# A four-layer graph network on one core: leaky slope, row sums, squares, degrees and scaling moved between VectorE, ScalarE and GpSimd, with new settings for the planner

## The chip, the cores and the metric

The kernel runs on one core of a Trainium2 chip. The metric is the device time of one execution in microseconds (us), the median of three runs. The core's engines work side by side, each through its own queue in order: TensorE (PE in the profile) multiplies matrices, VectorE (DVE) does elementwise work and reductions, ScalarE (ACT) evaluates functions with a scale and a bias per partition, GpSimd (POOL) does elementwise work on small or unhurried tiles, and SyncE (SP) issues the transfers (DMA).

## The reference: what is computed

Sixty-four graphs, each with 256 nodes of 512 features (`x`) and a weighted 256x256 adjacency matrix (`adj`), all in float32, pass through four layers. Every layer normalises, rectifies, calls a graph operator and adds the result to x:

```
h = maximum(layernorm(x), 0);  x = x + attention(h, adj, W, a)
h = maximum(layernorm(x), 0);  x = x + gcn(h, adj, kernel, bias)
h = maximum(layernorm(x), 0);  x = x + masked(h, adj, kernel)
h = maximum(layernorm(x), 0);  x = x + sage(h, adj, W)

attention: Wh = h W;  e = leaky_relu(Wh a1 + (Wh a2)^T, 0.2)
           e = where(adj > 0.5, e, -9e15);  softmax;  elu(e Wh)
gcn:       dh = rsqrt(rowsum(adj + I));  relu(dh (adj+I) dh h kernel + bias)
masked:    relu(adj h kernel) * (any nonzero in the row of h's input)
sage:      relu([h, (adj h) / max(rowsum(adj), 1e-6)] W^T)
```

## The kernel before, in words

A graph fills two chunks of 128 partitions: `xs` holds x (128 x 2 x 512), `aT` the transposed adjacency matrix, `a_nat` the matrix as it lies in memory, from which the degrees are summed. The 64 graphs are independent, and several are under way at once.

**The planner.** The kernel isn't written in the order in which it runs. `graph(b)` records every instruction of a graph with `op(engine, us, function, reads, writes)`, where `us` is the author's duration for it. `Plan.add` multiplies this by the factor of its engine in `STRETCH` (L25). `Plan.place` (L69) then lays all recorded instructions out on a model of the engines and of the buffers: each has a due time, counted back from the due time of its graph (`APART` = 12 for each graph, L23 and L343) along what depends on it; an engine takes, of the instructions that can start soonest, an urgent one first and then the one that is due first. For PE, an instruction counts as ready only `SPARE` = 0.8 us after its inputs (L26, L110). `emit` writes the queues in the order of the starts in that layout. On the chip the queues run in this fixed order with the true durations; an instruction whose inputs are late holds up all that is behind it on its engine. SP's queue, with the transfers in it, is ordered in the same way.

**The stages of a graph.** `norm(l)` (L372) opens each layer: two `bn_stats` and `bn_aggr` on DVE (L381, L383), `rstd` by an addition and a power on POOL (L385, L387), in layer 1 a product with `dh` on DVE (L390), `nb` = -mean times rstd on DVE (L392), and two Relu on ACT that write `h` (L396). `aggregate` (L424) multiplies h with the adjacency matrix or the attention into PSUM (`pt`). `left_sums` and `more_sums` build seven operands `xw` from it, and `project` (L485) multiplies them with seven prepared weights `wb` in a seven-product scheme with three PSUM banks (`pz`, `py`, `pv`; all at L503). Between products ACT copies bank z out (`snap`, L542) and DVE adds the others (L544). `pieces` lists the three parts in which the result comes, and `elu0`, `relu_add` and `masked` add them to `xs` on DVE.

Layer 0 has a stage of its own ahead of `aggregate`: four products with row sums on DVE (L590) give the logits `lg`, `along` brings one of them to all partitions through memory (`pl`, two dependent transfers), ACT adds the other (`e`, L596), and then come the leaky slope (L603), the mask as a product (L605) and as an addition of `off` (L607), the maximum (L610), the exponential with its sum (L614), the reciprocal (L617) and the scaling by it (L620). Degrees are summed on DVE (L576).

Layer 3 transposes h by 32x32 blocks on DVE (`hb`, L722) and brings the blocks into place by 16 transfers on SP (`hw`, L727) before it multiplies.

The order of emission starts with the weights; the last one (`last_weight`, L306) is transposed on PE (L325), copied out of PSUM by ACT (L332), and its sums are made on POOL (L289).

Of the kernel before, what the change touches and what calls it, by code (L numbers as in the profile page):

```python
# [11 lines left out]
ALU = mybir.AluOpType  # L12
AX = mybir.AxisListType

P = 128
# [6 lines left out]
HOP = 0.25  # L22
APART = 12.0  # L23

STRETCH = {"DVE": 1.06, "ACT": 1.1, "POOL": 1.1, "PE": 1.0, "DMA": 1.0}  # L25
SPARE = 0.8  # L26

# [121 lines left out]
def kernel(  # L149
# [39 lines left out]
    class Tiles:  # L189
# [148 lines left out]
    def quarter(t, i, j):  # L338
        return t[:, i, j * OH : (j + 1) * OH]

    def graph(b):

        me = Tiles(str(b), APART * b)  # L343
        op, declare, together = me.op, me.declare, me.together

        def along(name, column, keys):
# [22 lines left out]
        op("DMA", 256, lambda g: nc.sync.dma_start(  # L369
            g["a_nat"], adj[b].rearrange("(c p) m -> p c m", p=P)), (), ["a_nat"])  # L370

        def norm(l, scale=None):  # L372

            st, mv, rs, nb, h = (f"{n}{l}" for n in ("stats", "mv", "rstd", "nb", "h"))
            declare(st, [P, NC, 6], tag="stats")
            declare(mv, [P, NC, 2], tag="mv")
            declare(rs, [P, NC], tag="rstd")
            declare(nb, [P, NC], tag="nb")
            declare(h, [P, NC, F], tag="h")
            for c in range(NC):  # L380
                op("DVE", 0.69, lambda g, c=c: nc.vector.bn_stats(g[st][:, c, :], g["xs"][:, c, :]),  # L381
                   XS[2 * c : 2 * c + 2], [f"{st}.{c}"])
                op("DVE", 0.18, lambda g, c=c: nc.vector.bn_aggr(g[mv][:, c, :], g[st][:, c, :]),  # L383
                   [f"{st}.{c}"], [f"{mv}.{c}"])
            op("POOL", 0.31, lambda g: nc.gpsimd.tensor_scalar_add(g[rs], g[mv][:, :, 1], EPS_LN),  # L385
               [f"{mv}.0", f"{mv}.1"], [rs])
            op("POOL", 0.72, lambda g: nc.gpsimd.tensor_tensor(g[rs], g[rs], minus_half, ALU.pow),  # L387
               [rs, "=half"], [rs])
            if scale is not None:
                op("DVE", 0.2, lambda g: nc.vector.tensor_tensor(g[rs], g[rs], g[scale], ALU.mult),  # L390
                   [rs, scale], [rs])
            op("DVE", 0.3, lambda g: nc.vector.scalar_tensor_tensor(  # L392
                g[nb], g[mv][:, :, 0], -1.0, g[rs], ALU.mult, ALU.mult),
               [f"{mv}.0", f"{mv}.1", rs], [nb])
            for c in range(NC):
                op("ACT", 0.81, lambda g, c=c: nc.scalar.activation(  # L396
                    g[h][:, c, :], g["xs"][:, c, :], AF.Relu, bias=g[nb][:, c : c + 1],
                    scale=g[rs][:, c : c + 1]), XS[2 * c : 2 * c + 2] + [nb, rs], [f"{h}.{c}"])
# [153 lines left out]
        def pieces(l):  # L552
            kept = f"c{l}"
            return (
                (1, "xs.10", lambda g: g[f"pz{l}"], [f"pz{l}"], lambda g: quarter(g["xs"], 1, 0), ["xs.10"], 256),
                (1, "xs.11", lambda g: g[kept][:, 2], [f"{kept}.11"], lambda g: quarter(g["xs"], 1, 1), ["xs.11"], 256),
                (0, "xs.0", lambda g: both(g[kept]), [f"{kept}.00", f"{kept}.01"], lambda g: g["xs"][:, 0, :], ["xs.00", "xs.01"], 512),
            )


# [3 lines left out]
        for q in range(P // Q):  # L564
# [10 lines left out]
        norm(0)  # L575
        op("DVE", 0.67, lambda g: nc.vector.tensor_reduce(g["deg"], g["a_nat"], AX.X, ALU.add),  # L576
           ["a_nat"], ["deg"])
        op("POOL", 0.36, lambda g: nc.gpsimd.tensor_scalar_add(g["dh"], g["deg"], 1.0), ["deg"], ["dh"])
        op("POOL", 0.72, lambda g: nc.gpsimd.tensor_tensor(g["dh"], g["dh"], minus_half, ALU.pow),
           ["dh", "=half"], ["dh"])  # L580
        op("DVE", 0.18, lambda g: nc.vector.tensor_scalar_max(g["rdeg"], g["deg"], EPS_DEG),
           ["deg"], ["rdeg"])
        op("DVE", 0.18, lambda g: nc.vector.reciprocal(g["rdeg"], g["rdeg"]), ["rdeg"], ["rdeg"])
# [11 lines left out]
        for c in range(NC):  # L595
            op("ACT", 0.47, lambda g, c=c: nc.scalar.activation(  # L596
                g["e"][:, c, :], g["pl"], AF.Identity, bias=g["lg"][:, 1, c : c + 1]),
               ["pl", f"lg.1{c}"], [f"e.{c}"], urgent=True)
        E = ["e.0", "e.1"]
        declare("off", [P, NC, N])  # L600
        op("DVE", 0.48, lambda g: nc.vector.tensor_scalar(
            g["off"], g["aT"], 0.5, NEG_INF, ALU.is_le, ALU.mult), ["aT"], ["off"])
        op("DVE", 0.69, lambda g: nc.vector.scalar_tensor_tensor(  # L603
            g["e"], g["e"], ALPHA, g["e"], ALU.mult, ALU.max), E, E)
        op("DVE", 0.69, lambda g: nc.vector.scalar_tensor_tensor(  # L605
            g["e"], g["aT"], 0.5, g["e"], ALU.is_gt, ALU.mult), E + ["aT"], E)
        op("DVE", 0.69, lambda g: nc.vector.tensor_tensor(g["e"], g["e"], g["off"], ALU.add),  # L607
           E + ["off"], E)
        declare("top", [P, NC])
# [9 lines left out]
        for c in range(NC):  # L619
            op("DVE", 0.37, lambda g, c=c: nc.vector.tensor_scalar_mul(  # L620
                g["e"][:, c, :], g["e"][:, c, :], g["den"][:, c : c + 1]),
               [f"e.{c}", f"den.{c}"], [f"e.{c}", "e"])
        aggregate("h0", "e", 0)


        def elu0(i, key, y, y_keys, to, to_keys, n, tag):
# [10 lines left out]
            op("DVE", us, lambda g: nc.vector.scalar_tensor_tensor(  # L637
                to(g), g[ex], -1.0, to(g), ALU.add, ALU.add), [ex] + to_keys, to_keys)

# [28 lines left out]

        def relu_add(i, key, y, y_keys, to, to_keys, n):
            op("DVE", 0.43 if n == 256 else 0.69, lambda g: nc.vector.scalar_tensor_tensor(  # L670
                to(g), y(g), 0.0, to(g), ALU.max, ALU.add), y_keys + to_keys, to_keys,
               urgent="pz3" in y_keys)

        first, second, third = pieces(1)

        def last1(pz):
            declare("v1", [P, OH], tag="ex256")
            op("DVE", 0.49, lambda g: scaled(g, 1, g["v1"], g[pz], 0), [pz, "dh", "=bias"], ["v1"], urgent=True)
            relu_add(1, "xs.10", lambda g: g["v1"], ["v1"], first[4], first[5], 256)

        project([Weighted("xw1", 1)], 1, scaled_keep, 0.49, scaled_total, last1, ["dh", "=bias"])
        relu_add(*second)
        relu_add(*third)
        norm(2)

# [12 lines left out]

        def masked(i, key, y, y_keys, to, to_keys, n, tag):
# [5 lines left out]
            op("DVE", 0.43 if n == 256 else 0.69, lambda g: nc.vector.tensor_tensor(  # L705
                to(g), g[v], to(g), ALU.add), [v] + to_keys, to_keys)

# [53 lines left out]
        for at, to, i in ((2, S3, 1), (3, S4, 0)):  # L761
# [3 lines left out]
        project([Weighted("hw", 3), Gathered("aT", "aw", "y")], 3, plain_keep, 0.38, plain_total,  # L765
                lambda _: relu_add(*pieces(3)[0]))
        _, second, third = pieces(3)
        relu_add(*second)
        relu_add(*third)
        op("DMA", 512, lambda g: nc.sync.dma_start(  # L770
# [9 lines left out]
    for b in range(B):  # L780
        graph(b)
    buffers = dict(
        xs=7, a_nat=1, ab=1, aT=6, h=3, mva=6, xw=5, c=3, off=1, junk=1, ex256=2, ex512=2,
        wa_col=1, turned=1, row=4, pl=2, pr=1, hb=1, ps=8,
    )
    for tag in ("stats", "mv", "rstd", "nb", "deg", "dh", "rdeg", "lg", "top", "den", "mask"):
        buffers[tag] = 6
# [34 lines left out]
```

## Time and profile before

| | us |
|---|---|
| median of the runs (lowest, highest) | 2857.97 (2857.74, 2859.51) |
| the profiled execution's own time | 2858.11 |
| its span, first to last instruction | 2856.3 |
| PE busy | 2807.5 (98% of the span) |
| DVE busy | 2317.2 (81%) |
| ACT busy | 1326.1 (46%) |
| POOL busy | 1098.4 (38%) |

The busy time of an engine says how much of the span it worked, not who waited for whom. Where one engine is full over a stretch, work of the others in that stretch is hidden behind it as long as it comes in time; where it isn't, the row of what it waited for names the releaser. A matmul of this kernel (128x128 by 128x256, float32) appears as two records.

### The profile page before, as it was taken

What the parts mean: (1) busy time and instruction counts of PE and PEld (TensorE: products, weight loads), DVE (VectorE), ACT (ScalarE), POOL (GpSimd) and SP (SyncE); (2) the same over time, 40 slices, a digit from 0 to 9 for tenths busy, and PEclk for the clock granted to TensorE, in tenths of its full rate; (3) what the DMA queues carried; (4) which work ended last, traced back from release to release, by engine and by line L of the source; (5) the groups of instructions that cost most, each with busy time, mean ns of one, the idle gap of its engine ahead of it and who ended that gap; (6) DMA issues with size and microseconds to landing.
All of it is one profiled execution on the core that took longest, in us unless ns stands there. A gap on an engine that the chain in (4) does not pass through costs nothing.

```text
span 2856.3 us, 41700 instructions
## 1 busy us (share of the span) xinstructions
PE 2807.5 (98%) x12968; PEld 2464.4 (86%) x12968; DVE 2317.2 (81%) x5904; ACT 1326.1 (46%) x2963; POOL 1098.4 (38%) x1691
## 2 busy tenths in 40 slices
PE   4999999999999999999999999999999999999998
PEld 3888888888888888888888888888888888888887
DVE  8888888888888888878888878888888888888764
ACT  4544444444454444444444444444444445444432
POOL 5443343343333433433433334434334344344331
PEclk9999999999999999999999999999999999999999
DMA  6122222222222222222222222222222222222111
GB/s 184 22 48 51 55 59 49 59 65 47 51 60 54 58 59 49 61 49 56 64 49 53 67 44 57 59 50 59 56 50 62 49 54 66 48 53 61 39 37 45
DMA packets 495052, 160.98 MB, mean 56 GB/s; under 512 B 424816, under 2 KB 460656, under 8 KB 494832
## 3 DMA queue, kind: packets, MB, share of 16 engines
q1 hardware_dynamic: 494832, 158.33, 23.5%
q8 instruction: 104, 1.70, 0.3%
q14 instruction: 116, 0.95, 0.1%
HBM read 90.96 MB, written 33.69 MB: 44 GB/s over the span
## 4 chain that ended last, share of the span: by engine, by line
PE 97%; DVE 1%; SPq 1%; DMA 1%; ACT 0%; issue 0%; POOL 0%; DVEq 0%; ACTq 0%; POOLq 0%
PE pz L503 42%; PE pt L434 23%; PE pv L503 21%; PE py L503 11%; SPq L727 0%; DMA xs<-in_x_dram 0%; DMA wb<-in_L_gnn_W_dram 0%; ACT h L396 0%; DVE e L605 0%; DVE e L607 0%; SPq L567 0%; ACT e L614 0%; DVE stats L381 0%; DVE xs L670 0%; DMA hw<-hb 0%
## 5 line engine op out<-in xcount | busy, mean ns | idle before, releaser
L503 PE MATMUL pz<-wb,xw 128*128 128x256 f32 x3072 | 752.5, 379 | 0.9 <-ACT c L542 0.9
L503 PEld LDWEIGHTS pz<-wb,xw 128*128 128x128 f32 x3072 | 583.4, 190 | 80.7 <-ACT c L542 1.3
L503 PE MATMUL pz<-wb,hw 128*128 128x256 f32 x2048 | 524.5, 379 | 5.8 <-DMA hw<-hb 3.5
L406 POOL TENSOR_TENSOR xw<-xw 128x256 f32<-128x256 f32 x384 | 300.7, 803 | 536.1 <-DVE xw L402 443.3
L542 ACT COPY c<-pz 128x256 f32<-128x256 f32 x576 | 212.8, 370 | 591.7 <-PE pz L503 575.0
L503 PEld LDWEIGHTS pz<-wb,hw 128*128 128x128 f32 x2048 | 388.6, 190 | 60.9 <-issue 3.9
L396 ACT ACTIVATE h<-xs,nb,rstd 128x512 f32<-128x512 f32 x512 | 401.3, 811 | 60.0 <-DVE nb L392 59.9
L503 PE MATMUL pv<-wb,xw 128*128 128x256 f32 x1536 | 394.0, 379 | 0.0
L385 POOL TENSOR_SCALAR rstd<-mv 128x2 f32<-128x2 f32 x256 | 98.3, 384 | 698.2 <-DVE mv L383 325.7
L381 DVE BATCH_NORM_STATS2 stats<-xs 128x6 f32<-128x512 f32 x512 | 340.9, 681 | 6.9 <-DMA xs<-in_x_dram 5.2
L503 PEld LDWEIGHTS pv<-wb,xw 128*128 128x128 f32 x1536 | 291.8, 190 | 39.7
L544 DVE TENSOR_TENSOR c<-pv,c 128x256 f32<-128x256 f32 x384 | 161.0, 420 | 151.5 <-PE pv L503 112.8
L503 PE MATMUL pv<-wb,hw 128*128 128x256 f32 x1024 | 263.7, 380 | 0.0
L434 PE MATMUL pt<-e,h 128*128 128x256 f32 x1024 | 243.0, 382 | 20.9 <-ACT e L596 20.9
L434 PE MATMUL pt<-ahT,h 128*128 128x256 f32 x1024 | 237.5, 382 | 2.9 <-ACT b_w L332 2.9
L434 PE MATMUL pt<-aT,h 128*128 128x256 f32 x1024 | 238.5, 379 | 0.0
L434 PEld LDWEIGHTS pt<-e,h 128*128 128x128 f32 x1024 | 195.6, 191 | 48.7 <-ACT e L596 21.1
L434 PEld LDWEIGHTS pt<-ahT,h 128*128 128x128 f32 x1024 | 196.4, 192 | 30.3 <-ACT b_w L332 3.1
L503 PEld LDWEIGHTS pv<-wb,hw 128*128 128x128 f32 x1024 | 195.1, 191 | 26.7
L542 ACT COPY y<-pz 128x256 f32<-128x256 f32 x192 | 71.2, 371 | 316.4 <-PE pz L503 311.5
L434 PEld LDWEIGHTS pt<-aT,h 128*128 128x128 f32 x1024 | 194.6, 190 | 26.4
L387 POOL TENSOR_TENSOR rstd<-rstd,minus_half 128x2 f32<-128x2 f32 x256 | 200.6, 784 | 21.3
(103 smaller groups left out, 4411.0 us busy)
## 6 DMA issues: line engine op xcount, KB each, us to landing
xs<-in_x_dram SPq DMA_DIRECT2D x64, 512.0 KB
hw<-hb SPq DMA_DIRECT2D x1024, 32.0 KB
out_dram<-xs SPq DMA_DIRECT2D x64, 512.0 KB
ab<-in_adj_dram SPq DMA_DIRECT2D x512, 32.0 KB
a_nat<-in_adj_dram SPq DMA_DIRECT2D x64, 256.0 KB
pl<-dpl SPq DMA_DIRECT2D x64, 128.0 KB
pr<-dpr SPq DMA_DIRECT2D x64, 128.0 KB
w3n_w<-in_L_gnn_W_dram SPq DMA_DIRECT2D x4, 512.0 KB
```

Of the source, the lines that this page charges most:

```text
L381: op("DVE", 0.69, lambda g, c=c: nc.vector.bn_stats(g[st][:, c, :], g["xs"][:, c, :]), XS[2 * c : 2 * c + 2], [f"{st}.{c}"])
L385: op("POOL", 0.31, lambda g: nc.gpsimd.tensor_scalar_add(g[rs], g[mv][:, :, 1], EPS_LN), [f"{mv}.0", f"{mv}.1"], [rs])
L387: op("POOL", 0.72, lambda g: nc.gpsimd.tensor_tensor(g[rs], g[rs], minus_half, ALU.pow), [rs, "=half"], [rs])
L396: op("ACT", 0.81, lambda g, c=c: nc.scalar.activation(g[h][:, c, :], g["xs"][:, c, :], AF.Relu, bias=g[nb][:, c : c + 1], scale=g[rs][:, c ...
L406: op("POOL", 0.85, lambda g, i=i, o=o: nc.gpsimd.tensor_tensor(g[xw][:, o], g[xw][:, i], g[xw][:, S2], ALU.subtract), put(i, S2), put(o), ...
L434: nc.tensor.matmul(g[pt][:, kk, :], lhsT=g[h][:, c, k * P : (k + 1) * P], rhs=g[moving][:, c, :], start=(c == 0), stop=(c == NC - 1),)
L503: nc.tensor.matmul(g[t], lhsT=o.left(g, left, k), rhs=o.right(g, right, k), start=start and n == 0, stop=n == len(parts) - 1, skip_group_c ...
L542: return "ACT", lambda g, to, block: nc.scalar.copy(to, block)
L544: plain_total = (0.43, lambda g, i, to, block: nc.vector.tensor_tensor(to, block, to, ALU.add))
```

## The change: what it does

- **Leaky slope and mask.** The ACT instruction that adds the column now applies the parametric relu with slope 0.2 (L596), and the DVE instruction for the slope is gone. `off` becomes +0.5 or -0.5, and one DVE instruction takes the minimum of e and `off` times 1.8e16: three DVE instructions become one.
- **Row sums.** The DVE instructions that add a layer's result to `xs` also give the row sums of the new x (`accum_out` into `total`, a new tile), in layers 0 to 2. So `norm` of layers 1 to 3 has no `bn_stats` and no `bn_aggr`: POOL makes the negative mean from the sums (two instructions), and ACT squares x minus mean with a row sum (two instructions, whose elementwise result goes into `h` as scratch). Layer 0 keeps `bn_stats`.
- **Small products.** `nb` of layers 1 to 3 and the product with `dh` go from DVE to POOL.
- **Degrees and scaling.** The degrees are summed by two ACT copies with a row sum, `a_nat` written over itself; the attention is scaled by ACT.
- **Planner.** `STRETCH` is 1.25 for DVE, 1.15 for ACT and 1.2 for POOL; `SPARE` is 0.15; the due times of the last two graphs lie 0.3 x 12 us behind the one before each instead of 12. Three buffers for `ex256`, one for `pl`, six for `total`.

```diff
-STRETCH = {"DVE": 1.06, "ACT": 1.1, "POOL": 1.1, "PE": 1.0, "DMA": 1.0}
-SPARE = 0.8
+LAST, LATE = 2, 0.3
+STRETCH = {"DVE": 1.25, "ACT": 1.15, "POOL": 1.2, "PE": 1.0, "DMA": 1.0}
+SPARE = 0.15
...
-        me = Tiles(str(b), APART * b)
+        me = Tiles(str(b), APART * (b - (1.0 - LATE) * max(0, b - (B - 1 - LAST))))
...
+                op("POOL", 0.3, lambda g: nc.gpsimd.tensor_scalar(
+                    g[mv][:, 0, 1:2], g[t][:, 1:2], g[t][:, 2:3], -1.0 / F, ALU.add, ALU.mult),
+                   [f"{t}.10", f"{t}.11"], [f"{mv}.m1"])
+                op("POOL", 0.3, lambda g: nc.gpsimd.tensor_scalar(
+                    g[mv][:, 0, 0:1], g[t][:, 0:1], -1.0 / F, None, ALU.mult), [f"{t}.0"], [f"{mv}.m0"])
+                for c in (1, 0):
+                    op("ACT", 1.0, lambda g, c=c: nc.scalar.activation(
+                        g[h][:, c, :], g["xs"][:, c, :], AF.Square, bias=g[mv][:, 0, c : c + 1],
+                        accum_out=g[mv][:, 1, c : c + 1]),
+                       XS[2 * c : 2 * c + 2] + [f"{mv}.m{c}"], [f"{h}.{c}", f"{mv}.v{c}"])
+                op("POOL", 0.31, lambda g: nc.gpsimd.tensor_scalar(
+                    g[rs], g[mv][:, 1], 1.0 / F, EPS_LN, ALU.mult, ALU.add),
+                   [f"{mv}.v0", f"{mv}.v1"], [rs])
...
+        def into_x(l, key, at, us, fn, reads, to_keys, urgent=False):
+            t = f"total{l + 1}"
+            sums = l < 3
+            op("DVE", us + (0.1 if sums else 0.0), lambda g: fn(
+                g, dict(accum_out=g[t][:, at : at + 1]) if sums else {}),
+               reads + to_keys, to_keys + ([f"{t}.{key}"] if sums else []), urgent=urgent)
...
-        op("DVE", 0.67, lambda g: nc.vector.tensor_reduce(g["deg"], g["a_nat"], AX.X, ALU.add),
-           ["a_nat"], ["deg"])
+        for c in range(NC):
+            op("ACT", 0.66, lambda g, c=c: nc.scalar.activation(
+                g["a_nat"][:, c, :], g["a_nat"][:, c, :], AF.Copy, accum_out=g["deg"][:, c : c + 1]),
+               [f"a_nat.{c}"], [f"a_nat.{c}", f"deg.{c}"])
...
-                g["e"][:, c, :], g["pl"], AF.Identity, bias=g["lg"][:, 1, c : c + 1]),
+                g["e"][:, c, :], g["pl"], AF.Prelu, bias=g["lg"][:, 1, c : c + 1], alpha=ALPHA),
...
-            g["off"], g["aT"], 0.5, NEG_INF, ALU.is_le, ALU.mult), ["aT"], ["off"])
+            g["off"], g["aT"], 0.5, 0.5, ALU.is_gt, ALU.subtract), ["aT"], ["off"])
         op("DVE", 0.69, lambda g: nc.vector.scalar_tensor_tensor(
-            g["e"], g["e"], ALPHA, g["e"], ALU.mult, ALU.max), E, E)
-        op("DVE", 0.69, lambda g: nc.vector.scalar_tensor_tensor(
-            g["e"], g["aT"], 0.5, g["e"], ALU.is_gt, ALU.mult), E + ["aT"], E)
-        op("DVE", 0.69, lambda g: nc.vector.tensor_tensor(g["e"], g["e"], g["off"], ALU.add),
-           E + ["off"], E)
+            g["e"], g["off"], -2.0 * NEG_INF, g["e"], ALU.mult, ALU.min), E + ["off"], E)
...
-            op("DVE", 0.37, lambda g, c=c: nc.vector.tensor_scalar_mul(
-                g["e"][:, c, :], g["e"][:, c, :], g["den"][:, c : c + 1]),
+            op("ACT", 0.5, lambda g, c=c: nc.scalar.activation(
+                g["e"][:, c, :], g["e"][:, c, :], AF.Copy, scale=g["den"][:, c : c + 1]),
                [f"e.{c}", f"den.{c}"], [f"e.{c}", "e"])
```

More of the change, by code (lines that the diff above doesn't have):

```diff
@@ L369, in graph @@
         op("DMA", 256, lambda g: nc.sync.dma_start(
-            g["a_nat"], adj[b].rearrange("(c p) m -> p c m", p=P)), (), ["a_nat"])
+            g["a_nat"], adj[b].rearrange("(c p) m -> p c m", p=P)), (), ["a_nat.0", "a_nat.1"])
         def norm(l, scale=None):
-            st, mv, rs, nb, h = (f"{n}{l}" for n in ("stats", "mv", "rstd", "nb", "h"))
-            declare(st, [P, NC, 6], tag="stats")
-            declare(mv, [P, NC, 2], tag="mv")
+            mv, rs, nb, h = (f"{n}{l}" for n in ("mv", "rstd", "nb", "h"))
+            declare(mv, [P, 2, NC], tag="mv")
             declare(rs, [P, NC], tag="rstd")
@@ L379, in norm @@
             declare(h, [P, NC, F], tag="h")
[L380 to L386, printed above, removed]
+            if l == 0:
+                declare("stats", [P, NC, 6])
+                for c in range(NC):
+                    op("DVE", 0.69, lambda g, c=c: nc.vector.bn_stats(
+                        g["stats"][:, c, :], g["xs"][:, c, :]), XS[2 * c : 2 * c + 2], [f"stats.{c}"])
+                    op("DVE", 0.18, lambda g, c=c: nc.vector.bn_aggr(
+                        g[mv].rearrange("p a c -> p c a")[:, c, :], g["stats"][:, c, :]),
+                       [f"stats.{c}"], [f"{mv}.m{c}", f"{mv}.v{c}"])
+                op("POOL", 0.31, lambda g: nc.gpsimd.tensor_scalar(
+                    g[rs], g[mv][:, 1], EPS_LN, None, ALU.add), [f"{mv}.v0", f"{mv}.v1"], [rs])
+                sign = -1.0
+            else:
+                t = f"total{l}"
+                op("POOL", 0.3, lambda g: nc.gpsimd.tensor_scalar(
[8 more added lines that the diff above has]
+                       XS[2 * c : 2 * c + 2] + [f"{mv}.m{c}"], [f"{h}.{c}", f"{mv}.v{c}"])
+                op("POOL", 0.31, lambda g: nc.gpsimd.tensor_scalar(
+                    g[rs], g[mv][:, 1], 1.0 / F, EPS_LN, ALU.mult, ALU.add),
+                   [f"{mv}.v0", f"{mv}.v1"], [rs])
+                sign = 1.0
             op("POOL", 0.72, lambda g: nc.gpsimd.tensor_tensor(g[rs], g[rs], minus_half, ALU.pow),
@@ L389, in norm @@
             if scale is not None:
-                op("DVE", 0.2, lambda g: nc.vector.tensor_tensor(g[rs], g[rs], g[scale], ALU.mult),
+                op("POOL", 0.3, lambda g: nc.gpsimd.tensor_tensor(g[rs], g[rs], g[scale], ALU.mult),
                    [rs, scale], [rs])
[L392 to L395, printed above, removed]
+            if l == 0:
+                op("DVE", 0.22, lambda g: nc.vector.scalar_tensor_tensor(
+                    g[nb], g[mv][:, 0], sign, g[rs], ALU.mult, ALU.mult),
+                   [f"{mv}.m0", f"{mv}.m1", rs], [nb])
+            else:
+                op("POOL", 0.3, lambda g: nc.gpsimd.tensor_tensor(
+                    g[nb], g[mv][:, 0], g[rs], ALU.mult), [f"{mv}.m0", f"{mv}.m1", rs], [nb])
+            for c in (0, 1) if l == 0 else (1, 0):
                 op("ACT", 0.81, lambda g, c=c: nc.scalar.activation(
@@ L553, in pieces @@
             kept = f"c{l}"
+            if l < 3:
+                declare(f"total{l + 1}", [P, 3], tag="total")
             return (
-                (1, "xs.10", lambda g: g[f"pz{l}"], [f"pz{l}"], lambda g: quarter(g["xs"], 1, 0), ["xs.10"], 256),
-                (1, "xs.11", lambda g: g[kept][:, 2], [f"{kept}.11"], lambda g: quarter(g["xs"], 1, 1), ["xs.11"], 256),
-                (0, "xs.0", lambda g: both(g[kept]), [f"{kept}.00", f"{kept}.01"], lambda g: g["xs"][:, 0, :], ["xs.00", "xs.01"], 512),
-            )
+                (1, "10", lambda g: g[f"pz{l}"], [f"pz{l}"], lambda g: quarter(g["xs"], 1, 0), ["xs.10"], 256, 1),
+                (1, "11", lambda g: g[kept][:, 2], [f"{kept}.11"], lambda g: quarter(g["xs"], 1, 1), ["xs.11"], 256, 2),
+                (0, "0", lambda g: both(g[kept]), [f"{kept}.00", f"{kept}.01"], lambda g: g["xs"][:, 0, :], ["xs.00", "xs.01"], 512, 0),
+            )
+        def into_x(l, key, at, us, fn, reads, to_keys, urgent=False):
[4 more added lines that the diff above has]
+               reads + to_keys, to_keys + ([f"{t}.{key}"] if sums else []), urgent=urgent)
         declare("ab", [P, NC, N], tag="ab")
@@ L575, in graph @@
         norm(0)
-        op("DVE", 0.67, lambda g: nc.vector.tensor_reduce(g["deg"], g["a_nat"], AX.X, ALU.add),
-           ["a_nat"], ["deg"])
-        op("POOL", 0.36, lambda g: nc.gpsimd.tensor_scalar_add(g["dh"], g["deg"], 1.0), ["deg"], ["dh"])
+        for c in range(NC):
+            op("ACT", 0.66, lambda g, c=c: nc.scalar.activation(
+                g["a_nat"][:, c, :], g["a_nat"][:, c, :], AF.Copy, accum_out=g["deg"][:, c : c + 1]),
+               [f"a_nat.{c}"], [f"a_nat.{c}", f"deg.{c}"])
+        op("POOL", 0.36, lambda g: nc.gpsimd.tensor_scalar_add(g["dh"], g["deg"], 1.0), ["deg.0", "deg.1"], ["dh"])
         op("POOL", 0.72, lambda g: nc.gpsimd.tensor_tensor(g["dh"], g["dh"], minus_half, ALU.pow),
@@ L581, in graph @@
         op("DVE", 0.18, lambda g: nc.vector.tensor_scalar_max(g["rdeg"], g["deg"], EPS_DEG),
-           ["deg"], ["rdeg"])
+           ["deg.0", "deg.1"], ["rdeg"])
         op("DVE", 0.18, lambda g: nc.vector.reciprocal(g["rdeg"], g["rdeg"]), ["rdeg"], ["rdeg"])
@@ L619, in graph, with elu0 @@
         for c in range(NC):
-            op("DVE", 0.37, lambda g, c=c: nc.vector.tensor_scalar_mul(
-                g["e"][:, c, :], g["e"][:, c, :], g["den"][:, c : c + 1]),
+            op("ACT", 0.5, lambda g, c=c: nc.scalar.activation(
+                g["e"][:, c, :], g["e"][:, c, :], AF.Copy, scale=g["den"][:, c : c + 1]),
                [f"e.{c}", f"den.{c}"], [f"e.{c}", "e"])
         aggregate("h0", "e", 0)
-        def elu0(i, key, y, y_keys, to, to_keys, n, tag):
+        def elu0(i, key, y, y_keys, to, to_keys, n, at, tag):
             us = 0.42 if n == 256 else 0.61
@@ L636, in elu0 @@
                urgent="pz0" in y_keys)
-            op("DVE", us, lambda g: nc.vector.scalar_tensor_tensor(
-                to(g), g[ex], -1.0, to(g), ALU.add, ALU.add), [ex] + to_keys, to_keys)
+            into_x(0, key, at, us, lambda g, kw: nc.vector.scalar_tensor_tensor(
+                to(g), g[ex], -1.0, to(g), ALU.add, ALU.add, **kw), [ex], to_keys)
         first, second, third = pieces(0)
@@ L667, in graph, with relu_add @@
             to, block, g["dh"][:, i : i + 1], to, ALU.mult, ALU.add))
[L669 to L672, printed above, removed]
+        def relu_add(l, i, key, y, y_keys, to, to_keys, n, at):
+            into_x(l, key, at, 0.43 if n == 256 else 0.69,
+                   lambda g, kw: nc.vector.scalar_tensor_tensor(
+                       to(g), y(g), 0.0, to(g), ALU.max, ALU.add, **kw), y_keys, to_keys,
+                   urgent="pz3" in y_keys)
         first, second, third = pieces(1)
@@ L678, in last1 @@
             op("DVE", 0.49, lambda g: scaled(g, 1, g["v1"], g[pz], 0), [pz, "dh", "=bias"], ["v1"], urgent=True)
-            relu_add(1, "xs.10", lambda g: g["v1"], ["v1"], first[4], first[5], 256)
+            relu_add(1, 1, "10", lambda g: g["v1"], ["v1"], first[4], first[5], 256, 1)
         project([Weighted("xw1", 1)], 1, scaled_keep, 0.49, scaled_total, last1, ["dh", "=bias"])
-        relu_add(*second)
-        relu_add(*third)
+        relu_add(1, *second)
+        relu_add(1, *third)
         norm(2)
@@ L697, in graph, with masked @@
         aggregate("h2", "aT", 2)
-        def masked(i, key, y, y_keys, to, to_keys, n, tag):
+        def masked(i, key, y, y_keys, to, to_keys, n, at, tag):
             v = f"v2{tag}"
@@ L704, in masked @@
                urgent="pz2" in y_keys)
-            op("DVE", 0.43 if n == 256 else 0.69, lambda g: nc.vector.tensor_tensor(
-                to(g), g[v], to(g), ALU.add), [v] + to_keys, to_keys)
+            into_x(2, key, at, 0.43 if n == 256 else 0.69,
+                   lambda g, kw: nc.vector.scalar_tensor_tensor(
+                       to(g), g[v], 0.0, to(g), ALU.add, ALU.add, **kw), [v], to_keys)
         first, second, third = pieces(2)
@@ L765, in graph @@
         project([Weighted("hw", 3), Gathered("aT", "aw", "y")], 3, plain_keep, 0.38, plain_total,
-                lambda _: relu_add(*pieces(3)[0]))
+                lambda _: relu_add(3, *pieces(3)[0]))
         _, second, third = pieces(3)
-        relu_add(*second)
-        relu_add(*third)
+        relu_add(3, *second)
+        relu_add(3, *third)
         op("DMA", 512, lambda g: nc.sync.dma_start(
@@ L782 @@
     buffers = dict(
-        xs=7, a_nat=1, ab=1, aT=6, h=3, mva=6, xw=5, c=3, off=1, junk=1, ex256=2, ex512=2,
-        wa_col=1, turned=1, row=4, pl=2, pr=1, hb=1, ps=8,
+        xs=7, a_nat=1, ab=1, aT=6, h=3, mva=6, xw=5, c=3, off=1, junk=1, ex256=3, ex512=2,
+        wa_col=1, turned=1, row=4, pl=1, pr=1, hb=1, ps=8,
     )
-    for tag in ("stats", "mv", "rstd", "nb", "deg", "dh", "rdeg", "lg", "top", "den", "mask"):
+    for tag in ("stats", "total", "mv", "rstd", "nb", "deg", "dh", "rdeg", "lg", "top", "den", "mask"):
         buffers[tag] = 6
```

## The prediction

> **What bounds the kernel.** I read the busy times first, then the table by stretches, then who PE waited for, then the timeline at both ends.
>
> ```profile
> 200.00:2700.00 2500.00, 2500.00 (x11585) 2200.78 (x11584) 2058.99 (x5291) 1180.13 (x2637) 960.13 (x1493) 1.00 0.23 55
> ```
>
> The columns are the stretch, its length, busy time (and instructions) of PE, weight load, DVE, ACT and POOL, the granted PE clock, DMA share and GB/s. Over 2500 us PE is busy for 2500.00 at clock 1.00. Nothing that DVE, ACT or POOL give up there can be seen in the time, and the change leaves PE's products as they are. A graph costs PE 43.60 us (in the chain of waits the same product comes at 2263.52, 2307.12 and 2350.72), so 64 graphs cost 2790.4. Of the span of 2856.3, 65.9 us is something else, and it lies at the two ends:
>
> ```profile
> 60.00:70.00 10.00, 6.09 (x25) 4.91 (x26) 9.76 (x24) 7.26 (x19) 3.55 (x4) 0.74 0.11 43
> 2820.00:2840.00 20.00, 15.35 (x60) 11.94 (x58) 5.68 (x12) 2.07 (x6) 2.37 (x3) 0.91 0.25 54
> 2840.00:2857.00 17.00, 10.30 (x44) 8.11 (x44) 5.25 (x11) 1.28 (x4) 0.96 (x1) 1.00 0.08 31
> ```
> ```profile
> PE pt L434 <- ACT e L596: 20.9, 1, 20.9
> ...
> PE pz L503 <- DMA hw<-hb: 3.5, 1, 3.5
> PE pt L434 <- ACT b_w L332: 2.9, 1, 2.9
> PE pz L503 <- ACT c L542: 2.7, 5, 0.9
> ```
>
> The last fence is what PE waited for: total us, times, longest. From it and PE's timeline I make the ledger. Ahead of the first product of a graph: 36.4. The 32 transpose records of the last weight (L325): 3.5. Slow clock after the start: 16 records take 36.40 to 42.33 = 5.9, where 16 take 3.45 later: 2.5. Three gaps between 59 and 66 (0.76, 0.38, 2.90): 4.0. Slow clock behind them, 66.04 to 72.31 = 6.3 instead of 3.45: 2.8. Small waits up to 200 us: 1.4. At the end, a wait for the last graph's gather: 3.5, the slow clock behind it (12 records in 4.35 instead of 2.6): 1.8, five waits of 0.46 for ACT's copies: 2.3, and 4.9 after the last product. That is 63.1; the other 2.8 is mostly the pipelined end of the matmul ahead of each gap, which counts as busy.
>
> **The removed DVE work.** Per graph, by the groups: six `bn_stats` at 0.681 and six `bn_aggr` at 0.163: 5.06. L603, L605 and L607 (0.712, 0.783, 0.807) become one instruction of L605's kind: 2.30 - 0.78 = 1.52. Degrees 0.67; scaling 2 x 0.483 = 0.97; `nb` 3 x 0.175 and the product with `dh` 0.143: 0.67. Sum 8.89. Nine accumulator reads come in (L590's row: 0.081): 0.73. DVE falls from 36.2 to 28.0 of each 43.6.
>
> **What the others take.** ACT: six squares as L396, 0.811, with its read of the accumulator, 0.190: 6.0; two degree copies (no row; L596's 0.505, same elements, and 0.190): 1.4; two scalings 1.0. ACT goes from 20.7 to 29.1. POOL: six means, three `nb` and a product, each between L578's 0.309 and L385's 0.384: about 3.5; from 17.2 to 20.7. Both stay far under 43.6, behind a full PE; middle: **0**. If that cover were gone, the price is the exposed copy of the second rival below. The masked addition only changes its opcode (L705's 0.713 to L670's 0.697): 0. `norm` gets a longer chain: a POOL mean, 0.3 to 0.4, and square with read, 1.0, stand in place of `bn_stats` and `bn_aggr`, 0.84, about +0.5 us a layer, and the square waits in ACT's queue with the next Relu and bank copies behind it; in the middle other graphs' products cover this.
>
> The **parametric relu** isn't in this trace. Nearest row: L596, same operands, 0.505 against Identity. A table load is what could make it dearer:
>
> ```profile
> L281 ACT ACT_TABLE_LOAD x1 | 1.3, 1283 | 0.7 <-PEq L808 0.7
> ```
>
> One load serves Relu, Exp, Copy, Identity and Abs for the whole run. The Trainium skill (ScalarE: Activation LUTs, What ACT_TABLE_LOAD costs) says that each switch of function set costs 1.28 us of load and about 1.38 of drain; the load agrees with the row, the drain nothing here shows. If this relu isn't in exp's set, every graph switches twice: an estimate of 5.3 us of ACT a graph, ACT at 34.4 of 43.6, 1.3 to 2.7 us at places where the planner expects nothing. The page says that the cheap functions sit in every set but doesn't name this one. By the row: 0; by the rule, even one exposed load in four would be 32 x 1.28 = 41 us. I take 0, as a row with the same operands exists and relu is shared.
>
> **The start.** The first product waits for graph 0's softmax. `pl` lands at 26.26, and the DVE chain then stands in this queue:
>
> ```profile
> 28.30 0.68 DVE L576 TENSOR_REDUCE deg<-a_nat 128x2 f32<-128x512 f32 x1
> 29.32 0.71 DVE L570 STREAM_TRANSPOSE aT<-ab 128x512 f32<-128x512 f32 x1 [0.34 <-issue]
> 29.96 0.65 DVE L603 SCALAR_TENSOR_TENSOR e<-e 128x512 f32<-128x512 f32 x1
> 30.64 0.77 DVE L605 SCALAR_TENSOR_TENSOR e<-aT,e 128x512 f32<-128x512 f32 x1
> 31.44 0.82 DVE L607 TENSOR_TENSOR e<-e,off 128x512 f32<-128x512 f32 x1
> ```
>
> Two of the three go, 1.5, and the degrees ahead of them, 0.7: **-2.2**. The scaling swaps DVE for ACT at 0.5 each: 0. Bounds: with every link back to back from 26.3 (0.9 + 0.8 + 0.7 + 1.1 + 0.2 + 1.0 and hops) it would be 31.5, so -4.9; with the transpose of graph 1, which waits for its transfers, still ahead, or transfers in a worse order on SP, +1.
>
> **The ramp, 59 to 72 us, 6.8 lost.** DVE is 97% busy from 10 to 66 us, so it feeds PE. In that stretch go 4.2 (three graphs' mask work), 3.6 (L620, at 0.93 here), 1.4 (degrees) and some 3 of statistics: about 12 of 54. But the gap of 2.90 is released by ACT, at 65.63, behind four Relu and two exponentials, and ACT gains some 8 in these 66 us. So I take **half of it: -3.5**. Bounds: -7.5 (gaps, clock and the wait at 91), +4 if ACT's queue grows there.
>
> The slow clock is part of the size. The Trainium skill (TensorE: Matmul & The Clock Gate, Part 1) says that an idle window of about 3.4 us halves the clock, and as long a busy one restores it. Here 2.90, after two shorter gaps, was enough: granted 0.50 from 66 to 70. By the rule the gap costs 4.0, by the trace 6.8, so I use 6.8. The 0.46 gaps cost no clock.
>
> **The end.** Graph 63's sixteen gathers hold SP for 11 us, and PE finds nothing else:
>
> ```profile
> 2819.20 11.15 SPq L727 DMA_DIRECT2D hw<-hb  x16
> ...
> 2832.22 1.34 PE L503 MATMUL pz<-wb,hw 128*128 128x256 f32 x4 [3.48 <-DMA hw<-hb]
> ```
>
> Graph 62 had its gather issued 24 us earlier, at 2795.10. With due times 3.6 instead of 12 apart, the last graphs reach layer 3 close together: a gather takes SP 11.2, its multiplication 35 x 0.431 = 15.1 of PE, so gathers queued on SP stay ahead of PE. The 3.5 and the 1.8 go, and the last graph's copies remain exposed: **-5.0**. Late next is the last addition and the write, 4.9, which stays. Bounds: -7.8 (all waits); +6 if three gathers queue while PE has no other layer left.
>
> **Sum.** -2.2 - 3.5 - 5.0 = -10.7. Span 2845.6, plus 1.8 around it (2858.11 - 2856.3): 2847.4. The profiled execution stands 0.14 above the median, so **2847.3**, 0.37% less. A measurement can tell about 0.2%, 5.7 us: 2852.3 to 2863.7 would be no change.
>
> **Rivals.**
>
> *Only one end pays.* Transfers (DMA share 0.73 to 0.77 up to 50 us, two L325 gaps released by a transfer) hold the ramp: 2858.0 - 5.0 = 2853.0. Against it: DVE full there. Chance 0.14, half of it no change, half faster.
>
> *ACT makes PE wait* (slower). Place: bank z, whose next product waits for ACT's copy (L542); in the tail such a wait is seen bare, at 0.46. A square of 1.0 ahead of the copy in ACT's queue, with `SPARE` down from 0.8 to 0.15, leaves PE no margin. One exposed copy a graph: 64 x 0.46 = 29.4, less 10.7: 2877. It decides from 10.7 / 64 = 0.17 us a graph. For it: 15 copies a graph, ACT up by 40%. Against it: DVE at 81% empties the other banks without one wait in 2500 us, and ACT ends below that, at 67%. Chance 0.07 with the table load; another 0.05 that it only eats the gain (no change).
>
> *Both ends pay in full*: 4.9 + 7.5 + 7.8 = 20.2: 2838. The start leaves DVE as the feeder; but the transfers stay. Chance 0.16.
>
> Forecast 0.58. Faster: 0.58 + 0.16 + 0.07 and 0.03 of partly eaten gains = 0.84; same 0.09; slower 0.07. The range reaches from full pay to the one-ended case: 2837 to 2854.
>
> **What would show it.** First `pt` near 34; the gap near 63 shorter, with the clock row above 0.74; 200 to 2700 still full; the last gather issued before graph 62's products end; DVE near 1790, ACT near 1860 busy; one table load. It is wrong if PE shows waits for ACT's copies in the middle, or if the first product comes after 37.

## The result, and the profile after

The changed kernel takes 2844.11 us (2843.60 to 2844.22), against 2857.74 (2856.11 to 2859.51) for the kernel before on the same chip: a ratio of 0.9953 with a 95% interval of 0.9940 to 0.9967. The forecast was 2847.3 and the range 2837 to 2854. The profiled execution took 2844.11; its span is 2842.3, 14.0 us shorter than the 2856.3 of the profile before.

The table by stretches, with the columns as before, for the changed kernel:

```profile
200.00:2700.00 2500.00, 2499.59 (x11581) 2199.84 (x11580) 1742.63 (x4583) 1505.45 (x3666) 1084.91 (x2059) 1.00 0.24 55
60.00:70.00 10.00, 9.69 (x47) 8.20 (x46) 8.54 (x27) 8.69 (x19) 7.03 (x14) 1.00 0.40 90
2820.00:2843.00 23.00, 16.95 (x78) 14.25 (x76) 7.63 (x16) 2.49 (x7) 0.97 (x1) 0.92 0.12 46
```

The middle is as full as it was: PE has 0.41 us of gaps in 2500, while DVE's busy time there fell from 2058.99 to 1742.63 and ACT's rose from 1180.13 to 1505.45. The stretch from 60 to 70 us had 6.09 us of PE work at clock 0.74; now it has 9.69 at 1.00. Who PE waited for:

```profile
PE pt L460 <- ACT e L655: 15.8, 1, 15.8
...
PE pz L529 <- ACT c L568: 1.4, 3, 0.5
PE pv L529 <- DVE xw L445: 1.1, 1, 1.1
```

The rows for the last gather and for the weight's copies are gone. The first product of a graph starts at 33.20 instead of 36.40.

To give each place its share I count PE's records, since every graph costs 202 of them in 43.60 us, 0.216 each. This counts slow clock too, which busy time hides. The first 200 us of the kernel before, and then of the changed kernel:

```profile
0.00:200.00 200.00, 161.83 (x727) 137.97 (x728) 171.06 (x408) 97.26 (x217) 100.71 (x137) 0.98 0.32 85
```
```profile
0.00:200.00 200.00, 166.85 (x760) 142.18 (x761) 149.85 (x383) 129.50 (x320) 121.48 (x198) 1.00 0.35 90
```

The changed kernel is 33 records ahead at 200 us: 7.1 us. It loses 0.4 in the middle. The rest of the 14.0, **7.3 us**, is the end. There, PE's waits in the last 80 us of the changed kernel are one row:

```profile
PE pz L529 <- ACT c L568: 0.9, 2, 0.5
```

### The profile page after: what moved, and what is told of

The parts are those of the page before. It is cut to its first block, busy times and chain, and to the rows that moved or that the text cites. A ratio compares the mean times of both kernels' runs of the same rounds, so it can differ in the third digit from the quotient of the medians.

```text
span 2842.3 us, 43136 instructions
## 1 busy us (share of the span) xinstructions
PE 2802.9 (99%) x12968; PEld 2461.2 (87%) x12968; DVE 1963.5 (69%) x5136; ACT 1691.1 (59%) x4115; POOL 1246.4 (44%) x2331
## 4 chain that ended last, share of the span: by engine, by line
PE 97%; DMA 1%; DVE 1%; POOL 0%; SPq 0%; issue 0%; ACT 0%; DVEq 0%; POOLq 0%
PE pz L529 43%; PE pt L460 23%; PE pv L529 21%; PE py L529 11%; POOL wb L290 0%; DMA xs<-in_x_dram 0%; DMA ab<-in_adj_dram 0%; DVE e L628 0%; SPq L603 0%; DMA wb<-in_L_gnn_W_dram 0%; DVE e L642 0%; DMA pr<-dpr 0%; DVE xw L445 0%; SPq L259 0%; DVE stats L385 0%
## 5 line engine op out<-in xcount | busy, mean ns | idle before, releaser
L529 PE MATMUL pz<-wb,xw 128*128 128x256 f32 x3072 | 767.9, 379 | 2.5 <-DVE c L694 0.6
L401 ACT ACTIVATE h<-xs,mv 128x512 f32<-128x512 f32 x384 | 275.4, 718 | 56.1 <-POOL mv L395 36.3
L460 PE MATMUL pt<-e,h 128*128 128x256 f32 x1024 | 233.8, 381 | 15.8 <-ACT e L655 15.8
L409 POOL TENSOR_TENSOR rstd<-rstd,minus_half 128x2 f32<-128x2 f32 x256 | 215.9, 843 | 17.3
L628 DVE SCALAR_TENSOR_TENSOR e<-h,wa 128x512 f32<-128x512 f32 x256 | 196.7, 768 | 16.5 <-ACT h L422 5.8
L529 PE MATMUL py<-wb,xw 128*128 128x256 f32 x768 | 197.1, 379 | 0.0
```

Of the source, the lines that this page charges most:

```text
L401: op("ACT", 1.0, lambda g, c=c: nc.scalar.activation(g[h][:, c, :], g["xs"][:, c, :], AF.Square, bias=g[mv][:, 0, c : c + 1], accum_out=g[ ...
L460: nc.tensor.matmul(g[pt][:, kk, :], lhsT=g[h][:, c, k * P : (k + 1) * P], rhs=g[moving][:, c, :], start=(c == 0), stop=(c == NC - 1),)
L529: nc.tensor.matmul(g[t], lhsT=o.left(g, left, k), rhs=o.right(g, right, k), start=start and n == 0, stop=n == len(parts) - 1, skip_group_c ...
L628: op("DVE", 0.77, lambda g, j=j, c=c: nc.vector.scalar_tensor_tensor(g["e"].rearrange("p c n -> p (c n)"), g["h0"][:, c, :], 1.0, wa[:, j, ...
```

## The experiments

Two things were changed at once: instructions were moved between engines, and the planner was given other numbers, from which it makes another order of every queue. The theory: relief of DVE feeds the start, and the closer due times close the end. The rival: the new order does it. I first switched the planner's numbers, then kept the order fixed and exchanged the instructions.

**1. The due times alone, on the kernel before** (`e1_late_alone`).

```diff
+LAST, LATE = 2, 0.3
-        me = Tiles(str(b), APART * b)
+        me = Tiles(str(b), APART * (b - (1.0 - LATE) * max(0, b - (B - 1 - LAST))))
```

> The kernel before with nothing but the closer due times of the last two graphs. Theory (due times alone close the end, moved instructions feed the start): the queues start as before, first product at 36.4, and the end shortens by about 7 us, the gather wait of 3.5, its slow clock and most copy waits gone: about 2851. Rival (the end got shorter because the last normalisation no longer queues on VectorE): no gain here, 2858.

Measured: 2848.97 (ratio 0.9971, 0.9961 to 0.9982). In its last 80 us PE waits once, 0.5 us, for a copy. The last gather is issued at 2806.80, in a span of 2846.2; before it was 2819.20 in 2856.3. SP's queue, with issue time and duration:

```profile
2806.80 10.40 SPq L728 DMA_DIRECT2D hw<-hb  x16
```

Its span is 10.1 us shorter. `place` gives all instructions of the first half of this kernel the starts that they have in the kernel before, yet it has 735 records at 200 us and its first product at 35.19: 1.7 us of the 10.1 are the spread of the start between two executions of one order. The end's share is 8.4. So a start that is read from one profile can be off by some 1.7 us.

**2. The changed kernel without the closer due times** (`e2_no_late`).

```diff
-LAST, LATE = 2, 0.3
+LAST, LATE = 2, 1.0
```

> The changed kernel with due times 12 us apart to the end. Theory: start and ramp as in the changed kernel (first product at 33.2), the wait for the last gather returns, about +7: 2851. Rival: the end stays short, 2844 to 2846.

Measured: 2845.68, 1.6 more than the changed kernel: the number of the rival, not of the theory. The start is the same (762 records). The wait for the last gather comes back, but with 0.7 us instead of 3.5, and with no slow clock behind it:

```profile
PE pz L529 <- ACT c L568: 1.4, 3, 0.5
PE pz L529 <- DMA hw<-hb: 0.7, 1, 0.7
PE pz L529 <- ACT y L568: 0.5, 1, 0.5
```

So the due times are worth 8.4 us to the old kernel and some 2 to the new one, whose end is nearly closed without them. The rival's reason, the last normalisation, isn't shown by this: the order is another one too.

**3. The planner's factors and spare alone, on the kernel before** (`e3_plan_alone`).

```diff
-STRETCH = {"DVE": 1.06, "ACT": 1.1, "POOL": 1.1, "PE": 1.0, "DMA": 1.0}
-SPARE = 0.8
+STRETCH = {"DVE": 1.25, "ACT": 1.15, "POOL": 1.2, "PE": 1.0, "DMA": 1.0}
+SPARE = 0.15
```

> The kernel before with nothing but the new factors of the planner (1.25, 1.15, 1.2 and 0.15). Theory: the start needs the moved instructions, so first product at 36 and the ramp as long as before: 2858, give or take 3. Rival (another order of the same instructions is what closes the ramp): about 7 us less ahead of 200 us, 2851.

Measured: 3117.71, ratio 1.0915: 260 us slower, which neither theory had in it. The middle of this kernel:

```profile
200.00:2700.00 2500.00, 2371.91 (x10555) 2009.05 (x10554) 1930.84 (x4799) 1086.05 (x2403) 873.83 (x1356) 0.98 0.22 50
```

PE waits, and DVE is no busier than before (1930.84 against 2058.99). No engine is full: the order is what binds. The durations that the code gives for DVE's instructions sum to 41.2 us a graph; times 1.25 this is 51.5, more than PE's 43.7, so in the planner's layout DVE is the bound and PE waits for it. Times 1.06 it was 43.67, just below PE. The layout that `place` makes for this kernel ends at 3334, against 2860 for the kernel before; with DVE's factor alone changed it ends at 3336, with the other two alone at 2861. On the chip the three were not tried one by one. Among the largest waits of this kernel are those for things that this order brings late:

```profile
PE pt L434 <- ACT h L396: 67.8, 64, 3.1
PE pz L503 <- DVE c L659: 42.1, 42, 2.0
```

**4. The new spare alone, on the kernel before** (`g1_new_spare`: `SPARE` 0.15, the rest as before).

> The kernel before with the new spare of 0.15 and its old factors. If the 260 us that both new settings cost it come from the factors (VectorE's planned durations then sum to 51.5 us a graph, more than PE's 43.7): 2855 to 2860. If they come from the spare: above 2900.

Measured: 2858.28 (1.0006, 0.9998 to 1.0015), no difference. The 260 us come from the factors.

**5 and 6. The changed kernel with the old numbers.** `e4_old_plan` puts back factors and spare, `f2_old_stretch` the factors alone.

> The changed kernel with the old factors (1.06, 1.1, 1.1 and 0.8), due times as changed. Theory: the moved instructions still feed the start, 5 to 7 of its 7 us stay: 2844 to 2847. Rival: the start goes back to that of before, 2851.

> The changed kernel with the old factors of the engines and the new spare of 0.15. If the factors are what the long start with both old settings (2874) came from: 2870 to 2878. If the spare is: 2844 to 2848.

Measured: 2874.50 (1.0065, 1.0050 to 1.0080) and 2874.33 (1.0063, 1.0048 to 1.0078). With all instructions moved and the due times closer, the kernel is **slower than before**; the factors are the reason, not the spare. The first row is the start of `f2_old_stretch`, the others what PE waited for:

```profile
0.00:200.00 200.00, 151.61 (x641) 125.95 (x642) 131.65 (x356) 122.58 (x320) 107.67 (x180) 0.94 0.35 96
```
```profile
PE pt L460 <- ACT h L422: 9.1, 2, 4.7
PE pt L460 <- ACT b_w L333: 6.4, 1, 6.4
```

At 200 us it is 119 records, 25.7 us, behind the changed kernel, though its first product is early, at 31.82. Three times PE stands for 4.3 to 6.4 us in front of a product whose inputs aren't there, and each time the next sixteen records take 6.2 to 6.5 us instead of 3.45. The planner's own layout has this already: by the starts that `place` gives, 134.5 us of PE's work lie ahead of 200 us, against 154.8 in that of the changed kernel. The middle is full here as well (0.11 us of gaps). Of the 29.0 us between the two spans, 25.7 lie in the order of the start; most of the rest is at the end, where PE waits for seven copies instead of two.

**7. The order of the changed kernel, the work of the old one** (`u1_all_back`). What a planned instruction emits is exchanged; the planner sees the same durations, and every planned start is the same.

```diff
-        op("DVE", 0.69, lambda g: nc.vector.scalar_tensor_tensor(
-            g["e"], g["off"], -2.0 * NEG_INF, g["e"], ALU.mult, ALU.min), E + ["off"], E)
+        def three(g):
+            nc.vector.scalar_tensor_tensor(g["e"], g["e"], ALPHA, g["e"], ALU.mult, ALU.max)
+            nc.vector.scalar_tensor_tensor(g["e"], g["aT"], 0.5, g["e"], ALU.is_gt, ALU.mult)
+            nc.vector.tensor_tensor(g["e"], g["e"], g["off"], ALU.add)
+        op("DVE", 0.69, three, E + ["off", "aT"], E)
...
-            op("ACT", 0.66, lambda g, c=c: nc.scalar.activation(
-                g["a_nat"][:, c, :], g["a_nat"][:, c, :], AF.Copy, accum_out=g["deg"][:, c : c + 1]),
+            op("ACT", 0.66, lambda g, c=c: nc.vector.tensor_reduce(
+                g["deg"], g["a_nat"], AX.X, ALU.add) if c else None,
...
+                def both_stats(g, c):
+                    nc.vector.bn_stats(g[st][:, c, :], g["xs"][:, c, :])
+                    nc.vector.bn_aggr(g[mv].rearrange("p a c -> p c a")[:, c, :], g[st][:, c, :])
...
+                    op("ACT", 1.0, lambda g, c=c: both_stats(g, c),
```

> The changed kernel with every queue position as the planner gave it, but the moved work put back: at the place of the one mask instruction stand the old three, at the place of the degree copies the old sum on VectorE, the scaling, the statistics and the small products on VectorE as before. Theory (relief of VectorE feeds the start): the 7 us at the start go, most of the end stays, about 2851, and the middle stays full. Rival (the order of the queues is what closes the start): 2844 to 2847, start within 2 us of the changed kernel.

Measured: 2856.04 (0.9998, 0.9989 to 1.0006), as slow as the kernel before. The start and the middle:

```profile
0.00:200.00 200.00, 160.26 (x716) 133.80 (x717) 172.94 (x424) 96.04 (x218) 98.80 (x140) 1.00 0.32 85
```
```profile
200.00:2700.00 2500.00, 2498.33 (x11574) 2202.37 (x11573) 2125.41 (x5269) 1165.73 (x2630) 946.64 (x1495) 1.00 0.24 55
```

44 records fewer by 200 us than the changed kernel, 9.5 us, and 11 fewer than the kernel before; 1.3 us more gaps in the middle. So the new order is worth nothing at the start without the moved work, and there the rival falls in this form. The theory's 2851 was missed too, as the start lost more than 7.

The end is another matter. The two losses, 10.8, are nearly all of the 11.1 us between the two spans, so the end is as short as that of the changed kernel, and PE's waits in the last 80 us are the same:

```profile
PE pz L531 <- ACT c L570: 0.9, 2, 0.5
```

With the closer due times the end closes with the old work in it, in the old order (`e1_late_alone`) and in the new one. It doesn't need the last normalisation off VectorE.

**8. The order of the old kernel, the work of the changed one** (`v1_old_order`), the same exchange the other way. The squares' scratch is a fixed tile here, not `h`.

> The kernel before with every queue position as the planner gave it, but all of the work moved as in the change (one mask instruction, sums with the additions, squares, degrees and scaling on ScalarE, small products on GpSimd). Theory: the start gains 5 to 7 us without a new order: 2851. Rival: the fixed order keeps the waits where they were, first product at most 2 us earlier, 2855 to 2858.

Measured: 2852.48 (0.9986, 0.9979 to 0.9993), between the two. It has 746 records at 200 us: 4.1 us ahead of the profiled kernel before, 2.4 ahead of `e1_late_alone`, which has the same order there. At the end PE's gap shrinks from 3.48 to 2.71:

```profile
2827.48 1.10 PE L524 MATMUL pz<-wb,hw 128*128 128x256 f32 x4 [2.71 <-DMA hw<-hb]
```

The four records take 1.10 us, so the clock stays up this time; before, four took 1.34 and the next four 1.91. The gap is not shorter by an earlier gather: in both kernels it is issued 9.5 us before PE runs out of work, and here SP needs 10.40 us for it instead of 11.15. That this comes from the moved work isn't shown; `e1_late_alone` has 10.40 with the old work, `u1_all_back` 11.39.

**9 to 11. The parts of the relief, one at a time, in the changed kernel's order.** `u2_mask_back` puts back the mask work alone, `u3_deg_back` degrees and scaling, `u4_stats_back` the statistics with the small products.

> The changed kernel in its own order, with the three old mask and slope instructions at the place of the one. All of the moved work put back cost 9.5 us of products by 200 us (44 records). If the chain ahead of the first products matters most, this is the largest share, 4 to 6 us: 2848 to 2850. If it is VectorE's total load that matters, its share is 1.5 of 8.9, under 2 us: 2845 to 2846.

> The changed kernel in its own order, with the sum of the degrees and the scaling of the attention back on VectorE. By the chain: the scaling stands right ahead of the first product, 2 to 4 us: 2846 to 2848. By the load: 1.6 of 8.9, under 2 us.

> The changed kernel in its own order, with bn_stats, bn_aggr and the small products of layers 1 to 3 back on VectorE. By the chain: they come only from layer 1 on, behind the first products, so 1 to 3 us: 2845 to 2847. By the load: 5.8 of 8.9, the largest share, 5 to 6 us: 2849 to 2850.

| put back | median us | records at 200 us | us of start lost | DVE work a graph, us (as in the prediction) |
|---|---|---|---|---|
| nothing (changed kernel) | 2844.11 | 760 | 0 | 0 |
| mask and slope | 2848.32 | 745 | 3.2 | 1.5 |
| degrees and scaling | 2846.23 | 744 | 3.5 | 1.6 |
| statistics, small products | 2847.12 | 750 | 2.2 | 5.0 net |
| all | 2856.04 | 716 | 9.5 | 8.2 net |

The parts of the start, 8.9, nearly sum to the whole. They don't follow the amount of DVE work: the mask costs 2.1 us of start for each us of work, the statistics 0.4. By the medians it is 4.2, 2.1 and 3.0 us for the three, so the order of the last two isn't certain (the first sixteen records of products alone take between 5.20 and 6.45 us in the traces of the changed kernel, `u2_mask_back` and `u4_stats_back`), but the statistics stay far below their share of the work. What counts is what an instruction stands in front of.

For the mask it is not the first product, which comes at 33.49 instead of 33.20. It is the mask of the next graph, in front of an operand (`xw`) that PE needs; in the changed kernel this `xw` starts at 41.20:

```profile
40.08 1.65 DVE L644 SCALAR_TENSOR_TENSOR e<-e 128x512 f32<-128x512 f32 x1
41.76 0.69 DVE L645 SCALAR_TENSOR_TENSOR e<-aT,e 128x512 f32<-128x512 f32 x1
42.48 0.69 DVE L646 TENSOR_TENSOR e<-e,off 128x512 f32<-128x512 f32 x1
43.09 0.41 DVE L445 TENSOR_TENSOR xw<-pt,xw 128x256 f32<-128x256 f32 x1
43.65 2.04 PE L529 MATMUL pv<-wb,xw 128*128 128x256 f32 x4 [3.04 <-DVE xw L445]
```

PE's gap there is 3.04 instead of 1.13, and the clock is low behind it: four records in 2.04 instead of 1.10.

In `u3_deg_back` it is the first product, to be seen on DVE just before it:

```profile
32.65 0.69 DVE L613 TENSOR_REDUCE deg<-a_nat 128x2 f32<-128x512 f32 x1 [0.21 <-DMA a_nat<-in_adj_dram]
33.26 1.12 DVE L640 TENSOR_SCALAR off<-aT 128x512 f32<-128x512 f32 x1
34.30 0.34 DVE L655 TENSOR_SCALAR e<-e,den 128x256 f32<-128x256 f32 x1
34.78 1.19 PE L460 MATMUL pt<-e,h 128*128 128x256 f32 x2 [16.92 <-DVE e L655]
```

The degrees and the mask operand `off` of the next graph stand ahead of the scaling that the first product needs: 34.78 instead of 33.20. In the changed kernel the scaling waits as well, on ACT behind the degree copies of the next graph, which wait for the transfer of `a_nat`:

```profile
31.84 0.42 ACT L613 ACTIVATE a_nat<-a_nat 128x256 f32<-128x256 f32 x1 [1.91 <-DMA a_nat<-in_adj_dram]
32.66 0.89 ACT L655 ACTIVATE e<-e,den 128x256 f32<-128x256 f32 x2
```

The reciprocal that the scaling reads was done at 31.09, so some 1.5 us are still lost in front of the first product. In `f2_old_stretch` the scaling comes ahead of these copies, and the first product is at 31.82.

**12. A neighbour of the new spare** (`h1_spare01`: 0.1 instead of 0.15).

> The changed kernel with a spare of 0.1 instead of 0.15, nothing else. If the start depends on relief alone: 2844, no change. If it depends on the order, a small step of a setting can move it by several us either way.

Measured: 2842.96 (2842.52 to 2843.12), 1.15 below the changed kernel, with no gap in the middle and one copy wait fewer at the end; the start is the same (761 records). It is the fastest version run. The two ranges don't touch, but they come from different series, and 1.15 is under the 0.2% that a measurement of this kernel can tell.

## Why the prediction was right

**The bound.** That PE is full in the middle and nothing there can be won held: 2499.59 of 2500, and both exchanges of work at a fixed order, which move DVE's busy time there by hundreds of us, change PE's gaps by 1.3 us at most. It held with the new factors as well: with the moved work DVE's planned load is 41.1 (32.9 x 1.25), below PE's 43.7. The new counts of buffers were never exchanged by themselves. In the layout of `place` they matter: with the old counts the changed kernel ends at 2891 instead of 2857, and no run shows what the chip makes of that.

**The start, -2.2.** Measured 3.2, 36.40 to 33.20, of which some 1 us is within the spread of the start. The mask chain ran at once, as the degrees and the next graph's transpose no longer stood ahead of it: the maximum ends at 28.74 instead of 32.99. Of these 4.25 us only 3.2 reached the first product, for the scaling then stood behind the degree copies. I had put the scaling at 0; degrees and scaling together moved the first product by 1.6.

**The ramp, -3.5.** The rest of the start is 7.1 - 3.2 = 3.9. The reason given, DVE as the feeder, is shown by `u1_all_back`. What the prediction didn't see is that relief alone gives 2.4 to 4.1 of the 7.1 in the old order; the rest needs an order made for it, and the moved work in an order made with the old factors is 86 records, 18.6 us, behind the kernel before. My 5.7 for start and ramp rested on relief alone, so that it came close to 7.1 is in part luck.

**The end, -5.0.** The mechanism held, the size was off: 7.3, close to the outer bound of 7.8. I left the copy waits standing; they went from five to two. The closer due times, which I named as the only cause, are enough alone: they close the end with the old work, in the old order and in the new one. But they are not the only cause: taken out of the changed kernel they cost about 2 of the 7.3, because the new order and the moved work together close most of the end without them. Which of these two does that isn't separated further than `v1_old_order` does it (a wait of 2.71 in the old order, 0.7 in the new one).

**The costs of the middle.** One table load in the whole run, and the parametric relu takes what Identity took, 0.500 against 0.505. The row was right; the rule of the Trainium skill (ScalarE: Activation LUTs, What ACT_TABLE_LOAD costs) had no case here:

```profile
L282 ACT ACT_TABLE_LOAD x1 | 1.3, 1283 | 0.7 <-PEq L845 0.7
L634 ACT ACTIVATE e<-pl,lg 128x256 f32<-128x256 f32 x128 | 57.9, 500 | 0.8 <-DVE e L628 0.5 <-DMA pl<-dpl 0.3
```

**Busy times.** I expected 1790 us of DVE and 1860 of ACT; the page says 1963.5 and 1691.1. The error is in the reading: I took durations of groups away from a busy time. The groups of DVE sum to 2609 us before, but it was busy for 2317, because records of instructions that follow each other overlap. The sum fell by 418, to 2191, and the overlap shrank too. Of the 522 that I expected of the sum, about 100 are missing: several unchanged instructions became longer, as the two of L787 (L750 before), from 0.461 to 0.625. Why wasn't tried; POOL is busier, at 44% instead of 38%. Nothing of this touched the time.

**The rivals.** ACT making PE wait fell: 0.41 us of gaps in the middle, with ACT at 60% there. The table load fell with it. That the change could be slower through the order of its own planner, as in `e4_old_plan`, was in none of my cases; the factors stood in the diff, and I gave them no cost.

## What to carry to other kernels

Where one engine is full over the middle, a change to the others is worth what it does at both ends, and there an instruction counts more by what is queued behind it than by its length. When a change moves work and also changes what orders the queues, exchange the work at a fixed order and the order at fixed work: here neither half was worth as much alone, and the new factors alone cost 260 us. Before the settings of a planner are changed, sum its planned load of each engine against that of the bound, and look where its own layout ends. The sum alone would have missed `f2_old_stretch`, where DVE's planned load is only 34.9; the layout shows both losses, with ends at 3334 and 2878 against 2860 for the kernel before and 2857 for the changed one.

## What the runs showed of the hardware that was not expected

The length of one gap doesn't tell whether the clock of PE drops. It held through a gap of 2.71 us (`v1_old_order`) and dropped after one of 3.48 (before, to 0.50), each with two gaps of 0.46 ahead of it. But it also dropped after 2.90 (before), after 3.04 (`u2_mask_back`), and after 2.07 in `f2_old_stretch`, where gaps of 0.55 and 0.46 lay ahead: four records took 2.04 us, at 0.53. The Trainium skill (TensorE: Matmul & The Clock Gate, Part 1) has an idle window of about 3.4 us; the first two gaps agree with that, the other three don't, and what decides there is open.

A degree copy on ACT took 0.411, less than the 0.505 of the same size with a scale by partition, and a square 0.718, less than the 0.809 of the Relu with both scale and bias by partition: 0.09 for each such operand in both pairs, as the Trainium skill has it (ScalarE: Activation LUTs, What ACT_TABLE_LOAD costs).

```profile
L613 ACT ACTIVATE a_nat<-a_nat 128x256 f32<-128x256 f32 x128 | 52.5, 411 | 6.9 <-DMA a_nat<-in_adj_dram 6.9
L655 ACT ACTIVATE e<-e,den 128x256 f32<-128x256 f32 x128 | 61.0, 505 | 0.7 <-DVE den L652 0.7
L401 ACT ACTIVATE h<-xs,mv 128x512 f32<-128x512 f32 x384 | 275.4, 718 | 56.1 <-POOL mv L395 36.3 <-POOL mv L398 12.5 <-PE pt L460 6.2
```
